# Where a graph kernel's first count matrix is built, and how its rows' beginnings are found

## The chip, the cores and the metric

The kernel runs on one core of one Trainium2 chip. Its metric is the device time of one execution in microseconds; of several runs the median is given. A profile shows one further execution, with each engine's instructions: PE (TensorE matmul; PEld is its weight load), DVE (VectorE), ACT (ScalarE), POOL (GpSimd) and SP (SyncE, which here only issues transfers).

## The reference, cut to what matters

A four-layer graph network on 6250 nodes and 100000 edges sorted by destination. Destinations are drawn as 6250 u^2, so the low nodes have by far the most edges.

```python
h = relu(layernorm(x))                                       # 6250 x 256
deg = segment_sum(ones, dst)
h1 = h @ W1_self + (segment_sum(h[src], dst) / max(deg, 1)) @ W1_neigh + b1     # 256 -> 512
hp = relu(h1 @ W2_pool + b2_pool)
h2 = h1 @ W2_self + segment_max(hp[src], dst) @ W2_neigh + b2
h3 = ((segment_sum(h2[src], dst) + h2) / (deg + 1)) @ W3_neigh + b3
h4 = h3 @ W4_self + (segment_sum(h3[src], dst) / max(deg, 1)) @ W4_neigh + b4
out = x + h4 @ W_fc + b_fc                                   # 6250 x 256
```

## The kernel before

Nodes are cut into 49 tiles of 128, edges into 782 columns of 128. Sums over edges are made in two ways. For the first eight tiles of destinations (H1 = 8, the hub) a **count matrix** A is built: how many edges go from each source to each destination; the sum is then a dense product of A with all 49 tiles of h, which lie in SBUF as Z1 (three bf16 parts of each number). For the other tiles (d = 8 to 48) each edge column is **gathered**: `sums` issues on POOL one indirect transfer per column (L386) from the table tab_h in DRAM into a ring of 14 buffers, PE multiplies it by a one-hot matrix in three matmuls (L404) into pg, and DVE adds pg, masked by M, to acc (L421, L423), of which there are three. When a tile's sum is whole, `done1` finishes it: deg and the mean (L818 to L822, the mean m1 on ACT), transposes, the product with Wa and Wb (L838, L841), and stores of tab_t and tab_p. Layer 2 begins with gathers from tab_p (L1144), and needs all of it.

`build` (L297 to L331) makes A for one tile. The tile's 128 destinations are 16 **windows** of 8. A window's edges lie one after the other in the sorted list and fill up to k_of[w] rows of 128 edges: 31 for the first window, 14 for the next, then 11, 9, 8, 8; 139 rows for tile 0, 67, 52, 48, 48, 43, 32, 32 for tiles 1 to 7. One row is one **run**: ACT makes a one-hot matrix of the source's place in its tile, by Abs and Relu (L309, L311), DVE a mask of source tile and destination (hm, L313), and PE multiplies them (L319). At the end of a window DVE takes the maximum (L323) and ACT copies the counts into A (L324).

A `Hub` is a list of such work: `advance(to)` emits items up to number `to`, and the one-hot matrices four runs (LOOK) ahead.

**The beginning of the program, the prologue** (L533 to L802), has to find where each window's rows begin. The row number of window beginnings is found by a two-step search: how many of 128 equal pieces of the edge list end before the window (cF), then a gather of that piece of dst (drow, L621) and a count of what lies under the window's first node (L625). The 384 beginnings (three columns of SN) are turned into a row by PE (L631, starts), spread on POOL over at_row with a span for each k (33 spans; L653, L655), and turned back by PE into columns of row beginnings (L659, pa, atF, atI): 7 columns of 128 rows, of which the first 4 (RB1 = 512 rows) belong to the hub's eight tiles. Then `window_rows(b)` gathers 128 rows of dst and of src (L676), converts and transposes them, and `window_keys` makes of them the keys: sk (minus the source's place in its tile) and mk (what the mask is compared with). The first 512 go to sk1 and mk1; layer 2 reads the others from stash_k.

Beside this the prologue normalises x in seven groups of seven tiles (`layer_norm`, L568 to L594): statistics on DVE (L574, L575), Sqrt and Relu on ACT (L578, L584), the three bf16 parts by ACT (L587), DVE (L588), POOL (L589) and DVE (L590), and a store into tab_h. x is loaded into three buffers (xt). `turn` and `tail_keys` prepare the sources and keys of the gathered edges, `products1` multiplies weights.

**Layer 1** then emits, in this order: all of build 0; and, in `sums`, 474 gathers, behind each of which the hub advances in proportion. The hub's list is dense product 0 merged with build 1, dense 1 with build 2, and so on to dense 7. It ends with the last gather.

The order in the program is not the order in an engine's queue: the framework plans each engine's queue ahead, from estimated durations, by when an instruction's inputs should be there and, among those ready, by its place in the program. On the chip each queue then runs in that fixed order.

The kernel finds out at run time whether the input has the assumed shape (`bad`); a general path is taken otherwise, which does not run here.

Of the kernel before, what the change touches and what calls it, by code (L numbers as in the profile page):

```python
# [9 lines left out]
F32 = mybir.dt.float32  # L10
BF16 = mybir.dt.bfloat16
F16 = mybir.dt.float16
F8 = mybir.dt.float8e4
I32 = mybir.dt.int32
AF = mybir.ActivationFunctionType
ALU = mybir.AluOpType
AX = mybir.AxisListType
PSUM = bass.MemoryType.PSUM
DRAM = bass.MemoryType.DRAM

P = 128
# [4 lines left out]
G = 4  # L26
BLOCKS = (52, 100, 220, 180, 130, 100)
MERGED = 3
Z_SIGMA = 5.0
WIN = 8  # L30
# [48 lines left out]
def fast_path(  # L79
# [15 lines left out]
    nc = tc.nc  # L95
    N, FI = x.shape
    E = src.shape[0]
    FH = W1_self.shape[1]
    FO = W_fc.shape[1]
    NT = (N + P - 1) // P  # L100
# [234 lines left out]
    class Hub:  # L335
# [9 lines left out]
        def add(self, work):  # L345
            for w in work:
                if isinstance(w, tuple):
                    self.hot_at.append(len(self.work))
                else:
                    w = (None, w)  # L350
                self.work.append(w)

        def left(self):
            return len(self.work) - self.done

        def advance(self, to):
# [9 lines left out]

    def sums(pool, psg, table, F, srcT, keyT, jb, h, done, deep, hub, wait=0, counts=0, todo=()):

# [24 lines left out]
        for g in range(g_of[h][0], NG):  # L393
            pg = bank(psg, "pg", "pg", (F + counts,))
            n = min(G, T - g * G)
            for k in range(n):
                j = g * G + k
                X = ring[:, j % deep, :]
                gather(j)
                if j + ahead < T:  # L400
                    one_hot(j + ahead)
                for part in (2, 0, 1):
                    c = counts if part == 2 else 0
                    nc.tensor.matmul(  # L404
                        pg[:, : F + c], hot[j], X[:, part * F : (part + 1) * F + c],
                        start=(k == 0 and part == 2), stop=(k == n - 1 and part == 1),
                    )
                del hot[j]
                at = j - j0 + 1
                if at > wait:  # L410
                    hub.advance(math.ceil(len(hub.work) * (at - wait) / (T - j0 - wait)))
                if todo and next(todo[0], None) is None:
                    todo.pop(0)
# [102 lines left out]
    nc.gpsimd.memset(Z1[:, :, 3 * FI :], 1.0)  # L516
    for d in range(H1, NT):
        last = d == NT - 1
        ends = (g_of[d][0] * G * P, EX if last else (g_of[d][1] + 1) * G * P,
                offs[b_of[d][0]], EX if last else offs[b_of[d][1] + 1])  # L520
        for k in range(4):
            nc.gpsimd.memset(lim[:, k, d : d + 1], float(ends[k]))
    w1pool = layer1.enter_context(tc.tile_pool(name="w1", bufs=1))
# [6 lines left out]
    sk1 = w1pool.tile([P, RB1], F32, name="sk1")  # L530
    mk1 = w1pool.tile([P, RB1], F32, name="mk1")

    with ExitStack() as pro:  # L533
# [18 lines left out]
        def load_x(g):  # L552
            xt = lp.tile([P, LG, FI], F32, name="xt", bufs=3)
            i0 = g * LG
# [9 lines left out]

        for g in range(3):
            load_x(g)
# [28 lines left out]


        ones_b = ep.tile([P, 1], BF16, name="ones_b")
        nc.vector.memset(ones_b, 1.0)
        iota_n = ep.tile([P, 3 * P], F32, name="iota_n")
        nc.gpsimd.iota(iota_n, pattern=[[WIN, 3 * P]], base=0, channel_multiplier=0,  # L600
# [16 lines left out]
        within = ep.tile([P, 3], F32, name="within")  # L617
        drows = dflat[0:EP].rearrange("(p t) -> p t", t=T)
        for c in range(3):
            row = ep.tile([P, T], I32, name="drow", bufs=1)  # L620
            nc.gpsimd.indirect_dma_start(  # L621
                out=row, out_offset=None, in_=drows,
                in_offset=bass.IndirectOffsetOnAxis(ap=cI[:, c : c + 1], axis=0),
            )
            nc.vector.tensor_scalar(row, row, SN[:, c, 1:2], 0.0, op0=ALU.is_lt, op1=ALU.add,  # L625
                                    accum_out=within[:, c : c + 1])
        nc.vector.scalar_tensor_tensor(SN[:, :, 0], cF, float(T), within,
                                       op0=ALU.mult, op1=ALU.add)
        pr_ = bank(psm, "pm", "pr_s", (3 * P,))
        for c in range(3):  # L630
            nc.tensor.matmul(pr_[:2, c * P : (c + 1) * P], SN[:, c, :], ident,  # L631
                             start=True, stop=True)
        starts = ep.tile([2, 3 * P], F32, name="starts")
        nc.vector.tensor_copy(starts, pr_[:2, :])


        room = ep.tile([1, NW], F32, name="room")
        i = 0
        while i < NW:
            n = sum(1 for w in range(i, NW) if k_of[w] == k_of[i])  # L640
            nc.gpsimd.memset(room[:, i : i + n], float(k_of[i] * P))
            i += n
        has = ep.tile([1, NW], F32, name="hasw")
        nc.vector.tensor_sub(has, starts[:1, 1 : NW + 1], starts[:1, :NW])
        nc.vector.tensor_tensor(has, has, room, op=ALU.is_gt)
        nc.vector.tensor_reduce(bad[:1, 1:2], has, AX.X, ALU.max)


        at_row = ep.tile([2, RB * P], F32, name="at_row")
        nc.gpsimd.memset(at_row, 0.0)  # L650
        nc.gpsimd.memset(at_row[:1, :], float(E))
        for r, w0, n, k in spans:
            nc.gpsimd.tensor_copy(at_row[:, r : r + n], starts[:, w0 : w0 + n])  # L653
            if k:
                nc.gpsimd.tensor_scalar(at_row[:1, r : r + n], at_row[:1, r : r + n],  # L655
                                        float(k * P), None, op0=ALU.add)
        pa = bank(psm, "pm", "pa", (RB, 2))
        for b in range(RB):
            nc.tensor.matmul(pa[:, b, :], at_row[:, b * P : (b + 1) * P], ident[:2, :2],  # L659
                             start=True, stop=True)  # L660
        atF = ep.tile([P, RB, 2], F32, name="atF")
        nc.vector.tensor_copy(atF, pa)
        atI = ep.tile([P, RB], I32, name="atI")
        nc.vector.tensor_copy(atI, atF[:, :, 0])


        sk = ep.tile([P, RB * P], F32, name="skf")
        mk = ep.tile([P, RB * P], F32, name="mkf")
        skI = ep.tile([P, RB * P], I32, name="skI")
        dw = ep.tile([P, RB * P], F32, name="dwf")  # L670

        def window_rows(b):
            got = []
            for flat in (dflat, sflat):
# [10 lines left out]
            for i in range(2):  # L685
                nc.tensor.transpose(pt[:, i, :], f[:, i, :], ident)
            c = slice(b * P, (b + 1) * P)
            nc.vector.tensor_copy(dw[:, c], pt[:, 0, :])
            nc.vector.tensor_copy(mk[:, c], pt[:, 1, :])

        def window_keys(c0, c1):
            c = slice(c0, c1)
            nc.vector.tensor_copy(skI[:, c], mk[:, c])
# [89 lines left out]
        steps = products1()  # L783
        turn()
        for b in range(RB1 // P):
            window_rows(b)
        window_keys(0, RB1)
        nc.vector.tensor_copy(sk1, sk[:, :RB1])
        nc.vector.tensor_copy(mk1, mk[:, :RB1])
        for g in range(NT // LG):  # L790
            layer_norm(g)
            if g + 3 < NT // LG:
                load_x(g + 3)
            next(steps, None)
            if RB1 // P + g < RB:
                window_rows(RB1 // P + g)
        for _ in steps:
            pass
        tail_keys()
        window_keys(RB1, RB * P)  # L800
        nc.sync.dma_start(stash_k[:, 0, :], sk)
        nc.sync.dma_start(stash_k[:, 1, :], mk)  # L802


    with ExitStack() as on:
        pst = on.enter_context(tc.tile_pool(name="pst1", bufs=1, space=PSUM))
        psm = on.enter_context(tc.tile_pool(name="psm1", bufs=1, space=PSUM))
        psg = on.enter_context(tc.tile_pool(name="psg1", bufs=2, space=PSUM))
        psb = on.enter_context(tc.tile_pool(name="psb1", bufs=2, space=PSUM))
        psd = on.enter_context(tc.tile_pool(name="psd1", bufs=2, space=PSUM))  # L810
# [5 lines left out]
        def done1(d, acc):  # L816
# [23 lines left out]
            for k in range(KI):  # L840
# [6 lines left out]

        As = [wk.tile([P, NT, P], F8, name=f"A{i}", bufs=1) for i in range(2)]
        keys = (sk1, mk1, 0)
        todo = []  # L850
        builds = [build(d, As[d % 2], keys, wk, psb) for d in range(H1)]
        denses = [dense(range(NT), lambda s, A=As[d % 2]: A[:, s, :], h0_row, FI, psd,
                        lambda acc, d=d: todo.append(done1(d, acc)), extra=1)
                  for d in range(H1)]
        work = list(builds[0])
        first = len(work)
        for d in range(H1):
            work += merged(denses[d], builds[d + 1]) if d + 1 < H1 else denses[d]
        hub = Hub(work)
        hub.advance(first)  # L860
        todo.append(segments())
        sums(wk, psg, tab_h, FI, srcT, keyT, JC * P, H1, done1, 14, hub, counts=1, todo=todo)
    layer1.close()

# [1102 lines left out]
```

## Time and profile before

| | |
|---|---|
| median of 3 runs | 3042.52 us (3040.0 to 3048.64) |
| profiled execution | 3044.61 us, span 3042.8 us |
| busy share of the span | PE 81%, PEld 46%, DVE 67%, ACT 30%, POOL 67% |
| POOL's gathers of layer 1 (L386 from tab_h) | 474, 0.95 us each, from 148.9 to 785.9 us |
| first gather of layer 2 (L1144) | 824.5 us |
| first dense matmul (L442) | 267.0 us |

A line of a timeline gives the start, the duration, engine, source line, operation, output and inputs with shape, and in brackets how long the engine stood idle just before and what ended that. A line of windows gives, for a stretch, its length and, for each engine, the busy time and the number of instructions; PEclk is the granted clock of TensorE as a share of full speed. Matmuls overlap, so their durations add up to more than their distances.

### The profile page before, as it was taken

The page shows a single profiled execution, that of the slowest core. Times are in us where ns is not written, and L with a number is a line of the kernel's source. Part 1 is how long each engine was busy: PE and PEld are TensorE (multiplying, and loading weights), DVE is VectorE, ACT ScalarE, POOL GpSimd, SP SyncE. Part 2 cuts the span into 40 slices and gives each one's busy share as a digit, 9 for nine tenths or more (in the row PEclk, how much of TensorE's full clock was granted, in tenths as well). Part 3 has the DMA queues.
Part 4 walks back from the last instruction along what each step waited for, and adds up shares of the span by engine and source line. Part 5 has one row for each costly group of instructions (what it writes and reads, how often), then busy time and mean ns, then how long its engine had stood idle before and what let it go on. Part 6 is the DMA issues. An engine that isn't in the chain of part 4 may idle for free. (4 is left out here: it accounts for less than half of the span.)

```text
span 3042.8 us, 41553 instructions
## 1 busy us (share of the span) xinstructions
PE 2459.1 (81%) x12699; PEld 1402.3 (46%) x12699; DVE 2039.5 (67%) x5161; ACT 905.7 (30%) x2383; POOL 2051.3 (67%) x2260
## 2 busy tenths in 40 slices
PE   1468999999778664767789994983699999799999
PEld 0234666666543321323334442431234444488888
DVE  4956767766378788666779997987266676444433
ACT  2557766765255666421111110100000001000000
POOL 5274777776366676777767777765477777677775
PEclk9787999999999776788899997996799999899999
DMA  6454667776599999999989998987799999878886
GB/s 191 148 158 134 202 206 213 213 214 206 165 387 354 334 390 376 363 387 387 371 275 318 323 315 280 310 287 223 291 368 385 383 381 375 310 234 239 247 239 193
DMA packets 380021, 865.41 MB, mean 284 GB/s; under 512 B 58078, under 2 KB 151238, under 8 KB 379756
## 3 DMA queue, kind: packets, MB, share of 16 engines
q0 software_dynamic: 146560, 514.74, 51.8%
q1 hardware_dynamic: 175144, 292.49, 25.9%
q10 hardware_dynamic: 58084, 55.44, 5.8%
q8 instruction: 103, 1.69, 0.2%
q14 instruction: 130, 1.06, 0.1%
HBM read 610.65 MB, written 252.60 MB: 284 GB/s over the span
## 5 line engine op out<-in xcount | busy, mean ns | idle before, releaser
L1144 POOL DMA_INDIRECT X<-tab_p,srcIf x782 | 839.8, 1074 | 384.5 <-issue 161.5
L404 PE MATMUL pg<-ring,hot 128*128 128x256 bf16 (+2 forms) x3390 | 682.6, 310 | 78.3 <-DMA ring<-tab_h,srcT 34.8
L442 PE MATMUL pd<-zt,ac 128*128 128x256 bf16 (+1 forms) x3462 | 566.8, 299 | 21.6 <-DMA ac<-tab_a 12.2
L386 POOL DMA_INDIRECT ring<-tab_h,srcT x474 | 451.5, 952 | 195.8 <-PE pg L404 76.9
L404 PEld LDWEIGHTS <-hot 128*128 128x128 bf16 x3390 | 332.7, 99 | 303.1 <-issue 134.9
L442 PE MATMUL pd<-r,ae 128*128 128x512 bf16 x1536 | 378.5, 396 | 96.5 <-DVE acc L941 45.2
L386 POOL DMA_INDIRECT ring<-tab_r,srcE x342 | 330.6, 967 | 146.5 <-PE pg L404 63.6
L442 PEld LDWEIGHTS <-ac 128*128 128x128 fp8e4 x3462 | 339.4, 98 | 151.7 <-issue 21.0
L311 ACT ACTIVATE hs<-ht,onef 128x128 bf16<-128x128 bf16 x781 | 292.3, 395 | 305.3 <-PE pb L319 303.6
L319 PE MATMUL pb<-hm,hs 128*128 128x392 bf16 x781 | 257.4, 380 | 152.4 <-ACT A L324 109.4
L386 POOL DMA_INDIRECT ring<-tab_s,srcE x314 | 298.7, 951 | 112.8 <-issue 60.5
L423 DVE SCALAR_TENSOR_TENSOR acc<-pg,M,acc 128x257 f32<-128x257 f32 (+2 forms) x518 | 273.0, 561 | 151.4 <-PE pg L404 150.6
L1149 DVE SCALAR_TENSOR_TENSOR X<-X,samef 128x512 f32<-128x512 f32 x391 | 292.0, 748 | 97.6 <-DMA X<-tab_p,srcIf 84.0
L1149 DVE SCALAR_TENSOR_TENSOR X<-X,samef,X 128x512 f32<-128x512 f32 x385 | 287.2, 747 | 92.9 <-DMA X<-tab_p,srcIf 46.1
L442 PEld LDWEIGHTS <-ae 128*128 128x128 fp8e4 x1536 | 155.1, 101 | 330.4 <-issue 153.2
L382 DVE TENSOR_SCALAR hot<-iota_bf,keyE 128x128 bf16<-128x128 bf16 x656 | 153.5, 268 | 132.2 <-PE pg L404 126.0
L1083 PE MATMUL pm_prf<-unf,hTf 128*128 128x512 f32 x392 | 199.6, 637 | 2.8 <-ACT hTf L1074 2.8
L319 PEld LDWEIGHTS <-hs 128*128 128x128 bf16 x781 | 81.9, 105 | 249.5 <-issue 165.3
L442 PE MATMUL pd<-Z,A 128*128 128x256 bf16 (+1 forms) x1176 | 189.1, 274 | 0.3 <-ACT A L324 0.2
L313 DVE TENSOR_SCALAR hm<-iota_w,mk 128x392 bf16<-128x392 f16 x461 | 154.5, 344 | 46.0 <-PE pb L319 44.8
L324 ACT ACTIVATE A<-pb 128x392 fp8e4<-128x392 f32 x288 | 139.3, 486 | 147.7 <-DVE most L323 113.8
L323 DVE TENSOR_REDUCE most<-pb 128x1 f32<-128x392 f32 x288 | 160.8, 559 | 32.6 <-PE pb L319 31.9
(288 smaller groups left out, 2881.9 us busy)
## 6 DMA issues: line engine op xcount, KB each, us to landing
runb<-X SPq DMA_DIRECT2D x208, 512.0 KB
runb<-X SPq DMA_DIRECT2D x183, 256.0 KB
tab_r<-r SPq DMA_DIRECT2D x49, 384.0 KB
tab_a<-A SPq DMA_DIRECT2D x18, 784.0 KB
tab_t<-th SPq DMA_DIRECT2D x49, 256.0 KB
tab_p<-hpf SPq DMA_DIRECT2D x49, 256.0 KB
th<-tab_t ACTq DMA_DIRECT2D x49, 256.0 KB
X<-tab_p,srcIf POOLq DMA_INDIRECT x782
```

The source lines that it names most:

```text
L311: nc.scalar.activation(hots[0], t, AF.Relu, bias=one, scale=-1.0)
L313: nc.vector.tensor_scalar(hots[1], iota_w, mk[:, r : r + 1], None, op0=ALU.is_equal)
L319: nc.tensor.matmul(hold[0], hots[0], hots[1], start=(k == 0), stop=(k == k_of[w] - 1))
L323: nc.vector.tensor_reduce(most[:, w : w + 1], hold[0], AX.X, ALU.max)
L382: nc.vector.tensor_scalar(hot[j], iota_b, keyT[:, j - jb : j - jb + 1], None, op0=ALU.is_equal)
L386: nc.gpsimd.indirect_dma_start(out=ring[:, j % deep, : 3 * F], out_offset=None, in_=table, in_offset=bass.IndirectOffsetOnAxis(ap=srcT[:, ...
L404: nc.tensor.matmul(pg[:, : F + c], hot[j], X[:, part * F : (part + 1) * F + c], start=(k == 0 and part == 2), stop=(k == n - 1 and part == 1),
L423: nc.vector.scalar_tensor_tensor(acc[d], pg, m, acc[d], op0=ALU.mult, op1=ALU.add)
L442: nc.tensor.matmul(hold[0][:, : F + c], a, z[:, part * F : (part + 1) * F + c], start=(s == ss[0] and part == 2), stop=(s == ss[-1] and pa ...
L1083: nc.tensor.matmul(pm, hT[:, c, :], un[:, c, :], start=False, stop=(c == KH - 1))
L1144: nc.gpsimd.indirect_dma_start(out=X[:, k, :], out_offset=None, in_=tab_p, in_offset=bass.IndirectOffsetOnAxis(ap=srcI[:, t : t + 1], axis=0),
L1149: nc.vector.scalar_tensor_tensor(X[:, k, :], prev, same[:, t : t + 1], X[:, k, :], op0=ALU.mult, op1=ALU.max,)
```

## The change

Four things are different.

1. The search gathers the first of the three columns and counts it; the row beginnings of the first four columns are made from it alone. Row beginnings no longer pass through a row on one partition. A matrix win_of says for each row which window it belongs to; from it DVE makes for each column c of SN a selection matrix (1 where the row's window is that column's entry), and PE multiplies it with SN; a further matmul adds k times 128 for rows behind the first of a window, or the list's end for rows of no window. The second and third columns, and the last three columns of rows, follow after the first keys. The check that each window has room comes behind the second normalisation. The memsets of lim come behind `turn`, which itself comes later.
2. The keys sk1 and mk1 are made in place; stash_k gets only the others.
3. build 0 becomes a Hub `made` before the prologue. Behind each of the seven normalisations it advances by a seventh of its first 45 per cent (62 of 139 runs). Its matrix, one-hot buffers and PSUM banks are therefore there in the prologue, and x has two buffers in place of three.
4. In layer 1 the rest of build 0 heads the hub's list in `sums`, in place of standing ahead of the gathers, and the hub's pace is set so that it ends 24 gathers before the last.

```diff
+PART0 = 45
...
+        def rest(self):
+            at = set(self.hot_at[: self.hot])
+            return [(None if i in at else w[0], w[1])
+                    for i, w in enumerate(self.work) if i >= self.done]
...
-                    hub.advance(math.ceil(len(hub.work) * (at - wait) / (T - j0 - wait)))
+                    hub.advance(math.ceil(len(hub.work) * (at - wait) / (T - j0 - wait - rest)))
...
+    bpool = layer1.enter_context(tc.tile_pool(name="build1", bufs=1))
+    psb1 = layer1.enter_context(tc.tile_pool(name="psb1", bufs=2, space=PSUM))
+    As = [bpool.tile([P, NT, P], F8, name="A0", bufs=1)]
+    made = Hub(build(0, As[0], (sk1, mk1, 0), bpool, psb1))
+    part0 = len(made.work) * PART0 // 100
...
-            xt = lp.tile([P, LG, FI], F32, name="xt", bufs=3)
+            xt = lp.tile([P, LG, FI], F32, name="xt", bufs=2)
...
+        for r, w0, n, k in spans:
+            nc.gpsimd.iota(win_of[:, r : r + n], pattern=[[1, n]], base=w0,
+                           channel_multiplier=0, allow_small_or_imprecise_dtypes=True)
+            nc.gpsimd.memset(later[:, r : r + n], float(k * P))
...
+        def select(c):
+            nc.vector.tensor_scalar(sel[c], win_of[:, sel_at[c] : sel_at[c] + sel[c].shape[1]],
+                                    float(-c * P), pidx, op0=ALU.add, op1=ALU.is_equal)
+        select(0)
...
+        def row_begins(b0, b1, cs):
+            pa = bank(psm, "pm", "pa", (RB, 2))
+            for b in range(b0, b1):
+                for c in cs:
+                    nc.tensor.matmul(pa[:, b, :], sel[c][:, b * P - sel_at[c] : (b + 1) * P - sel_at[c]],
+                                     SN[:, c, :], start=(c == cs[0]), stop=False)
+                nc.tensor.matmul(pa[:, b, :], later[:, b * P : (b + 1) * P], unit,
+                                 start=False, stop=True)
+            nc.vector.tensor_copy(atF[:, b0:b1, :], pa[:, b0:b1, :])
+            nc.vector.tensor_copy(atI[:, b0:b1], atF[:, b0:b1, 0])
...
-        turn()
+        begins(0, 1)
+        row_begins(0, RB1 // P, (0,))
         for b in range(RB1 // P):
             window_rows(b)
-        window_keys(0, RB1)
-        nc.vector.tensor_copy(sk1, sk[:, :RB1])
-        nc.vector.tensor_copy(mk1, mk[:, :RB1])
+        window_keys(sk1, mk1)
+        select(1)
+        select(2)
+        begins(1, 3)
+        row_begins(RB1 // P, RB, (1, 2))
+        turn()
...
         for g in range(NT // LG):
             layer_norm(g)
-            if g + 3 < NT // LG:
-                load_x(g + 3)
+            if g + 2 < NT // LG:
+                load_x(g + 2)
             next(steps, None)
             if RB1 // P + g < RB:
                 window_rows(RB1 // P + g)
+            made.advance(part0 * (g + 1) // (NT // LG))
+            if g == 1:
+                check_room()
...
-        work = list(builds[0])
-        first = len(work)
+        work = []
         for d in range(H1):
             work += merged(denses[d], builds[d + 1]) if d + 1 < H1 else denses[d]
-        hub = Hub(work)
-        hub.advance(first)
+        hub = Hub(made.rest() + work)
         todo.append(segments())
-        sums(wk, psg, tab_h, FI, srcT, keyT, JC * P, H1, done1, 14, hub, counts=1, todo=todo)
+        sums(wk, psg, tab_h, FI, srcT, keyT, JC * P, H1, done1, 14, hub, counts=1, todo=todo, rest=24)
```

## The prediction

> **What bounds the kernel now.** I read the page first. Its chain of waits goes back only to 2121 us, so it says nothing about the beginning, where this change sits; that part has to be read from windows and from the queues' timelines. The windows in 25 us steps (columns: length, then busy time and count of PE, PEld, DVE, ACT, POOL, then the granted TensorE clock, DMA share, GB/s) show four regimes:
>
> ```profile
> 50.00:75.00 25.00, 3.63 (x12) 2.57 (x12) 8.56 (x18) 5.23 (x8) 17.18 (x32) 1.00 0.34 107
> 125.00:150.00 25.00, 7.63 (x22) 2.76 (x22) 25.00 (x116) 19.39 (x57) 3.79 (x4) 0.55 0.41 151
> 175.00:200.00 25.00, 15.46 (x78) 8.41 (x78) 14.07 (x48) 12.77 (x41) 19.02 (x20) 0.84 0.56 155
> 250.00:275.00 25.00, 19.07 (x65) 7.59 (x63) 13.10 (x38) 23.64 (x78) 0.97 (x2) 0.59 0.14 51
> 475.00:500.00 25.00, 24.73 (x180) 17.77 (x178) 19.79 (x72) 19.45 (x53) 18.91 (x21) 1.00 0.67 192
> ```
>
> At 50 to 75 us nobody works: DVE waits. From 100 us to the end of the prologue DVE is full. At 175 us layer 1's gathers run at POOL's rate (20 in 25 us, 1.25 us each) and PE has room. At 250 us the gathers have stopped and ACT is full. From 275 us on PE and POOL are both at their limit. The timelines of POOL, DVE and ACT name the turning points:
>
> ```profile
> 58.22 0.17 DVE L662 COPY atF<-pa 128x14 f32<-128x14 f32 x1 [14.82 <-PE pa L659]
> 59.42 3.82 POOL L676 DMA_INDIRECT wrow<-dflat,atI  x1 [0.67 <-DVE nb L582]
> 92.42 0.42 DVE L789 COPY mk<-mkf 128x512 f32<-128x512 f32 x1
> 140.83 2.02 DVE L590 TENSOR_TENSOR Z<-xt,Z 128x1792 bf16<-128x1792 f32 x1
> 148.88 0.97 POOL L386 DMA_INDIRECT ring<-tab_h,srcT  x1 [9.24 <-DMA tab_h<-Z]
> 267.08 0.93 ACT L822 ACTIVATE m<-acc,rmeanf 128x256 f32<-128x256 f32 x2
> 270.54 0.95 POOL L386 DMA_INDIRECT ring<-tab_h,srcT  x1 [23.99 <-PE pg L404]
> 824.51 0.97 POOL L1144 DMA_INDIRECT X<-tab_p,srcIf  x1 [37.63 <-DMA tab_p<-hpf]
> ```
>
> DVE stands 14.8 us at L662 for the row beginnings. The keys of the first 512 rows (sk1, mk1) are there at 92.8 us. The first gather waits for the last store of tab_h, behind the last L590. Build 0 then keeps ACT until 267 us; the copies m1 of finished sums stand behind it, with them the three acc buffers, the ring, and the gathers (24 us at 270.5). The last gather issues at 785.9 us, 37.6 us before layer 2's first. Layer 1's stage is thus 824.5 - 148.9 = 675.6 us; all behind it waits for tab_p and should move with it.
>
> **Part 1, the row beginnings.** Removed: three gathers of drow through one buffer (first issued 12.8 us, SN ready 36.3), and on POOL 33 copies and 31 additions into at_row, from 41.17 to 57.12 us. In their place one gather decides: it lands at 20.2, its count L625 takes 1.03, then eight small f32 matmuls (the L659 row: eight in 2.09 us) and two copies of 0.2: about 24.5 us instead of 59.1 for the first window gather. From it to mk1 took 92.8 - 59.4 = 33.4 us; the same again gives 58 us. Added: three selections, 512, 384 and 384 wide; the trace has no f16 to f32 form, but L699, two operations over 512 f32, takes 0.42 and over 384 0.35: 1.1 us of DVE; twice that if the form is slow. On POOL 33 iotas and 33 one-row memsets: L208's iota is 0.13, L205's 128x392 0.45, the lim memsets are 164 in 5.46, so about 27 x 0.13 + 6 x 0.24 + 33 x 0.04 = 6.3 us (up to 10, if each costs the 0.27 of a small addition on L655). They stand ahead of iota_n where the 5.46 us of lim stood, and iota_n (7.45) is not needed before dlast at 10.88: nothing to 1 us. The lim memsets go behind the window gathers, where POOL has slack (9.9 of 25 us busy at 75); without it, they delay one middle copy L589 by up to 5.5 us.
>
> **Part 2, the first 62 runs of build 0 in the prologue** (45% of 139, some nine behind each layer normalisation). A run costs ACT two activations at one per 0.29 us in a row (L309, L311 at 136 to 155 us): 0.585 us, 36 us in all. From 58 to 138 us ACT is busy some 34 of 80 now (5.2, 4.7, 16.0 and 8 in the windows), so it fits. DVE: 62 x 0.24 (L313, fifteen in 3.55) = 14.9, three reductions L323 of 0.56: 1.7, selections 1.1, less the copies L788 and L789 of 0.84: **+16.9 us**. DVE has 91.4 busy in the first 138 us, so 46.6 idle, of which 14.8 is the L662 wait that falls away and 7.5 (69.8 us) and 5.1 (89.0) are waits for window rows that now come while normalisations can fill them. If only the first is gained, the prologue grows by 2 us; if all are, it shrinks by 10. Should none be, it is 17.
>
> Against it stand two x buffers where there were three. The last group: statistics from 124.0, last L590 done at 142.8, 18.8 us; its load, 7 us for the first group (2.3 to 9.4), 11 for the last; and a chunk's 5.3 us of ACT and 2.2 of DVE may fall into the chain. A buffer is then held 33 to 37 us, with two of them a group each 17 to 18 us. Before, the L590s went from 38.6 to 140.8, 17.0 each. So the buffers allow what was there, hardly better: first store at 40, plus 6 x 17, plus the 6.1 us from last L590 to first gather, 148. Between 138 and 151 I take **147** for the first gather, 2 us earlier.
>
> Two rules of the Trainium skill speak against the move. The GPSIMD Engine Reference (8. Key points) says that GpSimd shares its SBUF interface with VectorE and suffers when the latter works in a two-port mode or with two SBUF inputs; L313, 16-bit with one source, may be of the first kind. The seven L589 took 1.67 to 2.08 us here; at the worst each for 0.4 more, 3 us, by the row nothing. I take nothing. TensorE: Matmul & The Clock Gate (Part 1: The HAM clock gate) says that the array runs at half rate, 1.2 GHz, without some 3.4 us of sustained work. Where it counts is the beginning of layer 1, below.
>
> **Part 3, layer 1.** 77 runs are left, followed by 392 dense and 322 other runs: 791 items over 474 - 24 = 450 gathers, 1.76 each. Build 0 is over at gather 44, so after 44 x 1.25 = 55 us, where it now takes until 267 us, 118 us after the first gather. ACT then needs 1.76 x 0.585 = 1.03 of each 1.25 us, and finished sums come from gather 36 on: the 24 us stall goes. PE needs, by the distance between starts in its timeline at 800 to 807 us, at full clock: 0.33 for a gather's three matmuls, 0.33 for a dense item, 0.163 for a run (392 columns in proportion to 0.33 for 3 x 257), 4.0 for the tile's end (0.33 + 0.23 + 1.72 + 1.72). In the first 44 gathers it has 0.33 + 1.76 x 0.163 = 0.62 each. By the row, the clock was 0.77 to 0.84 in this regime: 0.8 us, hidden. By the page's half rate (2.4 GHz halved, so 771 columns in 0.64 and 1.76 x 392 in 0.57) 1.22 of 1.25: just hidden. The sum is the same, with no margin by the page.
>
> Middle, 406 gathers: 0.33 + 392/406 x 0.33 + 322/406 x 0.163 + 45/406 x 4.0 = 1.22 us. The same prices give 500 us for what PE did between 275 and 808, where it took 533 (20 of it idle), so 1.25 to 1.30. POOL's floor is 1.25. Between them I take **1.29**, near the 1.30 that the gathers kept from 270 to 786: 524 us. Last 24: only sums and their ends, 24 x 1.25 = 30. After the last issue no dense backlog is left (22 us of it before, last L404 at 807.7): landing 3, one tile end of 10 instead of two in 16.7: 13. Sum 55 + 524 + 30 + 13 = 622, against 675.6.
>
> **The sum.** 147 + 622 = 769 for layer 2's first gather, 55.5 us earlier. The profiled execution had 3044.6 us, span 3042.8: it becomes 2989. It lay 2 us above the median of the runs, hence **2987**. The stores into stash_k that lose 512 of 896 columns, and the check of room, which now comes behind group 1, I cost at nothing: SP has slack at 109 us, and the verdict is read only ahead of the last layer; uncovered, its four DVE operations are 2.3 us.
>
> **The rivals.** *The prologue grows* (0.22). For: DVE is full from 100 us, and each queue's order is planned ahead, so a window row that lands late still stops everything. Against: the longest wait is gone. At 21 us per group: 40 + 126 + 6 = 172, plus 622, 794: 3012.
>
> *Both floors are reached* (0.12): first gather at 138, pitch 1.25 throughout, 605 us: 743, 81 us earlier, 2961. For: gathers kept exactly 20 per 25 us from 300 to 700. Against: PE was 99% busy there.
>
> *Slower* (0.10): two x buffers with no overlap. A load can't start until the last subtraction of the group two before, and that stands behind masks of build 0 which wait for PE and ACT. At 29 us per group 40 + 174 + 6 + 622 = 842, 17.5 later: 3060. It decides from (824.5 - 622 - 46)/6 = 26 us per group. Against: the last three L590s come 6 to 15 us after the one before.
>
> *It doesn't do what it says* (0.06): the order in which PE takes dense and sums leaves the backlog as it was and the pitch rises to 1.38, so the stage ends where it did: 3040.
>
> **How the numbers follow.** The forecast has 0.50, and 2970 to 3005 by its own bounds (first gather 138 to 155, pitch 1.25 to 1.31). The range takes in the grown prologue and the floors, 2958 to 3040, and leaves out the slower case and the far end of the faster. A change of 0.3%, 9 us, is about what a measurement of this kernel can tell from none. Faster beyond it are the forecast, the grown prologue and the floors, 0.84 less the part of the second that eats its gain: 0.82; within it 0.07; slower 0.11.
>
> **What would show it.** Right: the first window gather near 25 us; no long DVE wait for the row beginnings; first ring gather at 138 to 155; no gap of gathers; the first dense matmul some 55 us behind the first gather (267 us before); the last tile's end within 15 us of the last gather; layer 2 at about 769. Wrong: stores of tab_h on average more than 20 us apart, DVE or ACT waiting in the prologue for window rows or masks; gathers over 1.35 us apart in the middle; or a later stage that gives the gain back.

## The result, and the profile after

The changed kernel takes **3006.64 us** (median of four runs, 3002.8 to 3009.09) where the kernel before takes 3043.07 beside it: a ratio of **0.9885 [0.9867, 0.9902]**, 36 us less. The forecast was 2987, with 2958 to 3040 around it; the sign was right, and about two thirds of the forecast gain came. The profiled execution had 3004.22 us with a span of 3002.3, 40.5 us below the span before, and layer 2's first gather stands 39.7 us earlier: what lies behind layer 1 moved as one piece.

The windows of the changed kernel, in the columns used before (length, busy time and count of PE, PEld, DVE, ACT, POOL, then clock, DMA share, GB/s):

```profile
50.00:75.00 25.00, 22.72 (x72) 10.07 (x72) 22.00 (x69) 21.12 (x67) 3.69 (x3) 1.00 0.66 210
125.00:150.00 25.00, 10.73 (x25) 2.80 (x26) 25.00 (x100) 21.92 (x66) 1.83 (x2) 0.50 0.33 121
175.00:200.00 25.00, 17.49 (x78) 8.92 (x78) 13.46 (x46) 13.51 (x44) 18.91 (x21) 0.71 0.56 158
250.00:275.00 25.00, 22.89 (x149) 15.32 (x148) 16.01 (x56) 16.40 (x47) 18.90 (x21) 0.99 0.64 189
```

The hole at 50 to 75 us is filled: DVE is busy 22.0 of 25 us there, against 8.6. The hole of POOL at 250 to 275 is gone too: 21 gathers in place of two (0.97 us of POOL). In between nothing was won: from 100 to 150 us DVE is as full as before.

The turning points, from the timelines of POOL and DVE of the changed kernel:

```profile
10.32 5.68 POOL L833 MEMSET lim<- 1x1 f32 x164
16.52 1.10 POOL L651 DMA_INDIRECT drow<-dflat,cI  x1 [0.52 <-DVE wrongf L758]
28.67 0.17 DVE L675 COPY atF<-pa 128x8 f32<-128x8 f32 x1 [3.69 <-PE pa L673]
30.14 0.95 POOL L709 DMA_INDIRECT wrow<-dflat,atI  x1 [2.16 <-DVE mv L582]
50.71 0.68 DVE L735 TENSOR_TENSOR mk<-mk,dwf 128x512 f32<-128x512 f32 x1
143.48 2.01 DVE L597 TENSOR_TENSOR Z<-xt,Z 128x1792 bf16<-128x1792 f32 x1
151.79 0.98 POOL L393 DMA_INDIRECT ring<-tab_h,srcT  x1 [9.85 <-issue]
784.81 0.97 POOL L1187 DMA_INDIRECT X<-tab_p,srcIf  x1 [26.48 <-DMA tab_p<-hpf]
```

The window gathers start at 30.1 us (59.4 before), DVE's wait for the row beginnings is 3.69 us (14.82), and the keys mk1 are there at 51.4 (92.8). So the row beginnings come 29 us earlier and the keys 41 us earlier, and yet the first ring gather is 2.9 us *later*: 151.8 against 148.9. The whole gain lies behind it. Its 474 gathers run from 151.8 to 757.4 us without a stall (the longest wait is 2.3 us), 1.28 us apart (148.9 to 785.9 before, 1.35 on average with the stall), and from the last of them to layer 2's first it takes 27.4 us, where it took 38.6. Of the 39.7 us, 2.9 were lost in the prologue, 31.4 were won over the gathers and 11.2 behind the last one.

What DVE does in the prologue is seen in its groups between 50 and 143 us (busy time, then mean ns of one):

```profile
L314 DVE TENSOR_SCALAR hm<-iota_w,mk 128x392 bf16<-128x392 f16 x84 | 25.2, 351 | 0.0
L581 DVE BATCH_NORM_STATS2 st<-xt 128x6 f32<-128x256 f32 x35 | 13.3, 397 | 0.3 <-DMA xt<-in_x 0.3
```

These are 84 masks, not 62: the planner drew more than 20 runs of the part that is written behind the gathers forward into this stretch. And DVE waits only 0.3 us for x. It looks as if DVE were the bound of this prologue and its masks the reason. That was my first theory of the miss, and it fell.

### The profile page after: what moved, and what is told of

It reads as the page before. It is cut to its first block, busy times and chain, and to the rows that moved or that the text cites. A ratio compares the mean times of both kernels' runs of the same rounds, so it can differ in the third digit from the quotient of the medians.

```text
span 3002.3 us, 41497 instructions
## 1 busy us (share of the span) xinstructions
PE 2449.3 (82%) x12637; PEld 1403.4 (47%) x12719; DVE 2039.3 (68%) x5169; ACT 904.1 (30%) x2383; POOL 2035.2 (68%) x2260
## 5 line engine op out<-in xcount | busy, mean ns | idle before, releaser
L411 PE MATMUL pg<-ring,hot 128*128 128x256 bf16 (+2 forms) x3375 | 675.3, 309 | 79.2 <-DMA ring<-tab_h,srcT 36.2
L320 PE MATMUL pb<-hm,hs 128*128 128x392 bf16 x781 | 254.7, 375 | 150.3 <-ACT A L325 111.5
L310 ACT ACTIVATE ht<-iota_bf,sk 128x128 bf16<-128x128 bf16 x461 | 172.2, 395 | 6.5
```

What stands on the lines that cost most here:

```text
L310: nc.scalar.activation(t, iota_b, AF.Abs, bias=sk[:, r : r + 1])
L320: nc.tensor.matmul(hold[0], hots[0], hots[1], start=(k == 0), stop=(k == k_of[w] - 1))
L411: nc.tensor.matmul(pg[:, : F + c], hot[j], X[:, part * F : (part + 1) * F + c], start=(k == 0 and part == 2), stop=(k == n - 1 and part == 1),
```

## The experiments

Theory A: the first gather is late because DVE carries some 85 masks, 0.30 us each, ahead of the last store of tab_h. Theory B: it is late because two x buffers set the pace of the layer normalisations, and the masks lie in time that DVE has anyway. The experiments ran together on another chip, on which the kernel before takes 3453.88 us (3419.73 to 3475.4, 29 runs) and the gathers of layer 1 stand 1.75 to 1.84 us apart, so of their times only the ratios count, and lengths of layer 1 are compared among them alone. In the prologue the chips agree well enough for comparison (first window gather at 30.4 to 30.7 us with the new row beginnings, 30.1 above). The last of the four kernels below has the whole prologue of the change: its first gather is at 151.0 us, so on this chip that is the number to compare with. Neither the kernel before nor the changed kernel has a trace from this chip.

**The row beginnings alone.** Build 0 stays whole and ahead of the gathers, with three x buffers and the old pace:

```diff
-    As = [bpool.tile([P, NT, P], F8, name="A0", bufs=1)]
-    made = Hub(build(0, As[0], (sk1, mk1, 0), bpool, psb1))
...
-            xt = lp.tile([P, LG, FI], F32, name="xt", bufs=2)
+            xt = lp.tile([P, LG, FI], F32, name="xt", bufs=3)
...
-            made.advance(part0 * (g + 1) // (NT // LG))
...
-        hub = Hub(made.rest() + work)
+        hub = Hub(builds[0] + work)
+        hub.advance(len(builds[0]))
...
-        sums(wk, psg, tab_h, FI, srcT, keyT, JC * P, H1, done1, 14, hub, counts=1, todo=todo, rest=24)
+        sums(wk, psg, tab_h, FI, srcT, keyT, JC * P, H1, done1, 14, hub, counts=1, todo=todo, rest=0)
```

> The new row beginnings alone: build 0 stands whole ahead of the gathers as before the change, x has its three buffers, the hub's pace is the old one. Twelve masks stand ahead of the last store of tab_h in DVE's queue (six before the change, 85 with all of it). Theory A, the prologue is DVE's: with the 14.8 us wait gone and no masks added the first gather comes at 128 to 136 us, layer 1 then takes its old 676 us, and the whole 3022 to 3032 us. Rival B, the chain through the x buffers sets the first gather and the wait only hid in it: first gather at 146 to 150, the whole at 3040 to 3044.

Measured: ratio 0.9933 [0.9906, 0.996]. The timeline of POOL and the window behind it:

```profile
131.32 0.97 POOL L393 DMA_INDIRECT ring<-tab_h,srcT  x1 [9.47 <-DMA tab_h<-Z]
278.42 0.94 POOL L393 DMA_INDIRECT ring<-tab_h,srcT  x1 [36.50 <-PE pg L411]
...
250.00:275.00 25.00, 16.33 (x40) 4.01 (x40) 15.43 (x46) 25.00 (x85) 0.00 (x0) 0.50 0.00 1
```

The first gather is at 131.3 us, 17.6 ahead of the kernel before (whose trace is from the first chip). That is what the new row beginnings, with the keys made in place, are worth if nothing else is touched; the stores of tab_h then follow each other at 11.5 us on average. Build 0 still stops the gathers, for 36.5 us here, with ACT full and POOL empty. The prologue is as theory A has it, and B as it was put for this run (the x buffers set the first gather even when there are three) is out. That two buffers set it is still open, as there are three here.

**All but the row beginnings.** The old search through at_row, with the share in the prologue, two buffers and the new pace:

```diff
-        begins(0, 1)
-        row_begins(0, RB1 // P, (0,))
...
-        select(1)
-        select(2)
-        begins(1, 3)
-        row_begins(RB1 // P, RB, (1, 2))
...
+        for c in range(3):
+            row = ep.tile([P, T], I32, name="drow", bufs=1)
...
-            if g == 1:
-                check_room()
```

> All of the change but the new row beginnings: these are made on POOL as before, one drow buffer, starts, at_row. Theory A: DVE gets its 15 us wait back and the keys come some 35 us later, while 86 masks still stand ahead of the last store: first gather at 162 to 175, the whole at 3016 to 3030. Rival B (DVE is full from 76 us on anyway and would only be full later): first gather within 4 us of 152, the whole at 3004 to 3010.

Measured: ratio 0.9935 [0.9906, 0.9963], and

```profile
56.66 0.17 DVE L669 COPY atF<-pa 128x14 f32<-128x14 f32 x1 [14.82 <-PE pa L666]
179.37 0.98 POOL L393 DMA_INDIRECT ring<-tab_h,srcT  x1 [9.29 <-DMA tab_h<-Z]
...
1032.95 0.97 POOL L1155 DMA_INDIRECT X<-tab_p,srcIf  x1 [24.86 <-DMA tab_p<-hpf]
```

The first gather is 4 us beyond A's bracket, 23 us beyond the latest that B allowed, and 28 us behind that of the kernel with the whole prologue, so the early keys are needed: masks of build 0 start only at 82.8 us, and DVE is busy just 7.1 of the 25 us from 50 to 75. The third group's x was asked for at 39.5 us, but its statistics stand in DVE's queue among the window rows and masks, from 71.9 to 91.7 us, and its store comes 51.8 us behind the second's. From there on the stores follow at 15.4 us each (111.80 to 173.40), the pace of the changed kernel. Beside its late prologue, this kernel has the shorter layer 1: 853.6 us from its first gather to layer 2's, against 910.8 with the row beginnings alone. Each part by itself is worth 0.7%, one ahead of the first gather, the other behind it. Together they gave 1.1% on the first chip.

**No mask ahead of the last store.** PART0 is 0, and the masks of the remaining runs compare with a copy of mk1 that needs the last group of Z1, so that they can't be drawn forward:

```diff
-PART0 = 45
+PART0 = 0
...
+        mk1b = wk.tile([P, RB1], F32, name="mk1b", bufs=1)
+        nc.vector.scalar_tensor_tensor(mk1b, Z1[:, NT - 1, FI : 3 * FI], 0.0, mk1,
+                                       op0=ALU.mult, op1=ALU.add)
+        mk1s.append(mk1b)
```

> After the change, with no run of build 0 ahead of the last store of tab_h: the share is 0 and the masks compare with a copy of mk1 that waits for that store's data, so that the planned order can't draw them forward. 0 masks in place of 85, two x buffers. Theory A: 85 masks and five reductions, 28 us of DVE, are gone, first gather at 122 to 132; layer 1 has 92 runs more to do and its first dense matmul comes 90 us behind the first gather in place of 62; the stage takes 648 to 662 in place of 633, the whole 2994 to 3012. Rival B, two x buffers bind: first gather at 145 to 152, the whole at 3016 to 3032.

Measured: ratio 0.9911 [0.9879, 0.9943]. Its windows, and the rows of two groups' way through the buffers from the queues of SP, DVE, ACT and POOL:

```profile
75.00:100.00 25.00, 7.06 (x23) 3.35 (x22) 23.09 (x92) 11.28 (x19) 3.85 (x2) 0.68 0.32 108
100.00:125.00 25.00, 0.00 (x0) 0.00 (x0) 23.65 (x113) 10.89 (x18) 2.70 (x3) 0.50 0.55 177
125.00:142.30 17.30, 0.00 (x0) 0.00 (x0) 7.53 (x20) 5.44 (x9) 2.48 (x2) 0.50 0.31 107
```

```profile
100.33 0.36 SPq L601 DMA_DIRECT2D tab_h<-Z  x1
100.74 0.56 SPq L569 DMA_DIRECT2D xt<-in_x  x1
...
109.19 0.43 DVE L584 BATCH_NORM_STATS2 st<-xt 128x6 f32<-128x256 f32 x1
...
116.45 3.55 ACT L594 ACTIVATE xt<-xt,nb,rs 128x256 f32<-128x256 f32 x7 [0.53 <-DVE fhalf L478]
120.03 1.69 ACT L597 CAST Z<-xt 128x1792 bf16<-128x1792 f32 x1
122.03 2.02 DVE L598 TENSOR_TENSOR xt<-xt,Z 128x1792 f32<-128x1792 f32 x1
124.11 1.68 POOL L599 CAST Z<-xt 128x1792 bf16<-128x1792 f32 x1 [8.94 <-DVE fixIf L511]
125.83 2.02 DVE L600 TENSOR_TENSOR Z<-xt,Z 128x1792 bf16<-128x1792 f32 x1 [1.71 <-POOL Z L599]
...
142.29 2.03 DVE L600 TENSOR_TENSOR Z<-xt,Z 128x1792 bf16<-128x1792 f32 x1 [1.78 <-POOL Z L599]
150.25 0.97 POOL L395 DMA_INDIRECT ring<-tab_h,srcT  x1 [8.00 <-DMA tab_h<-Z]
```

Here theory A falls. All masks are gone from the stretch (the first one is at 145.1 us), and the first gather is at 150.3, not at 122 to 132: 0.8 us ahead of the kernel of this chip that has the masks (151.0). The second fence shows what sets the pace: the load of a group goes out when the last subtraction of the group two before has ended, 0.4 us behind that group's store in the same queue; its first statistics come 8.5 us later; then statistics, Relu, the three parts one after the other on ACT, DVE, POOL, DVE. From load to last part: 100.7 to 127.9, 27.1 us. Over all five groups that are loaded so, a buffer is held for 35.6, 33.0, 28.2, 27.1 and 25.0 us, 29.8 on average; two buffers share it, which is 14.9 us per group, where 15.1 was measured. The last parts stand at 87.70, 98.25, 116.34, 125.83 and 142.29, two groups in 26 to 29 us. DVE's full row did not show a bound: with the masks gone, the planner put small operations of a later stage (L476 to L518, lists of rows to mend) in their place, and from 100 to 125 us DVE was still busy 23.7 of 25 us, while PE had nothing at all to do. When these ran out, from 125 us to the start of the last part, it was busy 7.5 of 17.3 us, and the last group still came 16.5 us behind the one before. The first two holds are longer by more than load and stages: in the first the statistics begin only 15.4 us behind the load, and in the second it takes 24.2 us from them to the end of the last part, where the last group takes 15.0. So the masks are excluded as the cause; that DVE's other work took part in the pace up to 125 us is not.

In layer 1 this kernel pays for it: its first dense product comes 171.7 us behind the first gather, not 90, and there is again a stall, of 24.3 us, that ends at 338.6 us, with ACT busy 22.4 of the 26.6 us before. On that chip's slower gathers, its layer 1 is nevertheless within 4 us of the next kernel's (870.7 and 873.9).

What isn't tried: the direct test of theory B, three buffers against two with all else equal, for instance two buffers in the kernel with the row beginnings alone. That kernel has the same layer normalisations, three buffers, the new row beginnings and stores 11.5 us apart (the last four parts begin at 91.41, 101.14, 110.05 and 123.28); it differs from this one in the buffers and in build 0, which has no mask ahead of the last store here and some a few us ahead of it there. B is thus supported by these two runs and by the 15.4 us of the one before, but not shown by itself; A is excluded by one.

**The old pace of the hub.** The items are spread over all 474 gathers, the last 24 included:

```diff
-        sums(wk, psg, tab_h, FI, srcT, keyT, JC * P, H1, done1, 14, hub, counts=1, todo=todo, rest=24)
+        sums(wk, psg, tab_h, FI, srcT, keyT, JC * P, H1, done1, 14, hub, counts=1, todo=todo, rest=0)
```

> After the change with the hub's old pace: it ends with the last gather and not 24 ahead of it. If the pace shortens the stage's end: from the last gather to layer 2's first 34 to 40 us in place of 27, the last gather some 3 us earlier, the whole 3010 to 3016. Rival: PE has the same work in all and no idle time, so that the order at the end is worth nothing: within 3 us of the change, 3004 to 3010.

Measured: ratio 0.9922 [0.9892, 0.9953]. POOL's rows, and the end of PE's timeline:

```profile
151.02 0.97 POOL L393 DMA_INDIRECT ring<-tab_h,srcT  x1 [9.68 <-issue]
1024.95 0.97 POOL L1187 DMA_INDIRECT X<-tab_p,srcIf  x1 [37.62 <-DMA tab_p<-hpf]
```

```profile
1008.52 0.49 PE L449 MATMUL pd<-Z,A 128*128 128x257 bf16 x3
...
1017.00 1.98 PE L884 MATMUL pm_hp<-Wa,th 128*128 128x512 f32 x4 [1.46 <-ACT th L879]
1018.82 1.88 PE L887 MATMUL pm_hp<-Wb,th 128*128 128x512 f32 x4
```

POOL's wait is 37.62 us, as in the kernel before (37.63), where the kernels with the new pace had 24.8 to 26.5: dense products run until 1008.5, 22 us behind the last gather, and two tile ends follow them. So the pace alone is worth 11 to 13 us behind the last gather. The rival has it that this is paid for ahead of it, by a later last gather with the new pace. The kernel with the old row beginnings lets one see that: it has the new pace, about as many runs done before its first gather (92 against 90), and its first dense product as far behind it (84.8 and 84.9 us). Its gathers stand 1.750 us apart, against 1.766 with the old pace, so nothing was paid, and its layer 1 is 20.3 us shorter (853.6 against 873.9). By these two traces the rival falls on this chip, where PE has more room (busy 18.3 of 25 us at 475 to 500, against 24.7 in the kernel before on the first). That the last gather would come 3 us earlier with the old pace did not happen. In the time of the whole the step can't be told, since the intervals of all four kernels overlap.

## Why the prediction was right, and where it was off

**Row beginnings, 24.5 us: 30.1.** The work was priced well: the 33 iotas and 33 memsets took 3.42 to 9.60 us on POOL, 6.2 us with the waits in it (6.3 predicted), and from the first window gather to mk1 it took 21 us, less than the 33 of before. What failed first is "the lim memsets go behind the window gathers". Written behind, they were planned ahead: having no inputs, they were ready, so 5.7 us of them run from 10.3 us, and the gather of drow stands behind them at 16.5 (12.8 before). Not all of the 3.7 us are theirs: its row number cI was ready at 13.7 us rather than 12.5, as all three selections, two of them also written behind, ran 1.98 us on DVE from 8.84, ahead of the first statistics. The count of drow began at 23.1 us, where 20.2 was forecast: 2.9 of the missing 5.6 us. The second slip is in the matmuls. The "eight in 2.09 us" of L659 were four matmuls, since each of these f32 matmuls has two records; the new scheme has eight, and its 16 records took 4.2 us (24.46 to 28.63). On top of it DVE counted the second column (1.02 us) between the two copies.

**First gather, 147: 151.8.** It was right to a few us by luck: two errors cancel. The step said first store at 40, six groups of 17, and 6.1 behind. It came to 53.4 (the keys now stand on DVE ahead of the first group's parts, with the last mk row at 50.7), six groups of 15.4, and 6.3 behind the end of the last part. The pace was put down to DVE and buffers together; without a mask it is 15.1. The buffers are held 27 to 33 us (33.2, 29.3, 26.9, 31.1 and 30.2, 30.1 on average), not 33 to 37, and half of that is the pace. The +16.9 us of DVE were 62 masks; 84 ran. The kernel without them has its first gather 0.8 us earlier than the one with them on the same chip, so they cost hardly more than that (other work took part of their place). The slower rival, two x buffers without overlap at 29 us per group, and the grown prologue at 21, were both far from it; yet the slower rival's suspect, the buffers, fits the runs best: the kernel with three has its first gather at 131 us.

**First dense product 55 us behind the first gather: 62.** By the first gather 91 of 139 runs had been done rather than 62, so the smaller rest should have ended sooner. The term that failed is 1.76 items per gather: the 48 runs left went over 49 gathers, about one each, and in PE's timeline from 195 to 207 us most of them stand singly between the matmuls of two gathers, where PE waits 0.2 to 1.1 us at a time for the ring. Why they were queued so and not closer these runs don't show. No gather waited for it.

**The middle, 1.29 us a gather: 1.28.** 151.8 to 757.4 is 605.6 us, where 55 + 524 + 30 = 609 were predicted. The stall of 24 us is gone for the reason given: finished sums found ACT free (13.5 of 25 us busy from 175 to 200); both kernels that keep most of build 0 for after the prologue stall again, for 36.5 and 24.3 us. The clock weighed in this part was granted at 0.71 from 175 to 200 us, PE was busy 17.5 of 25 us, and POOL kept its 1.25: between the price by the row and that by the half rate of the Trainium skill (TensorE: Matmul & The Clock Gate, Part 1), both of which hid it. The other rule of the skill, on SBUF shared by GpSimd and VectorE (GPSIMD Engine Reference, 8. Key points), was looked for on the wrong engine. POOL's copies took no longer with ten times as many masks beside them: L596 1.68 to 1.95 us, those of before 1.67 to 2.08. But DVE's instructions did:

```profile
42.54 1.69 POOL L596 CAST Z<-xt 128x1792 bf16<-128x1792 f32 x1
42.23 2.09 DVE L716 CAST wrowf<-wrow 128x128 f32<-128x128 int32 x1 [0.18 <-DMA wrow<-sflat,atI]
82.04 1.65 DVE L589 SCALAR_TENSOR_TENSOR nb<-mv,rs 128x7 f32<-128x7 f32 x1
110.52 1.07 DVE L314 TENSOR_SCALAR hm<-iota_w,mk 128x392 bf16<-128x392 f16 x1
```

The same three forms take 0.18 to 0.23, 0.15 to 0.17 and some 0.3 us elsewhere in this prologue, and each of these three ends within 0.2 us of the end of a copy (44.23, 83.68 and 111.47 us). By that, DVE's full row holds waits of this kind too. What they cost in the end was not tested; the prediction looked for a loss at the copies alone and took nothing.

**Behind the last gather, 13 us: 27.4.** This is the term that cost most, 14.4 of the 15.8 us by which layer 2's first gather missed 769; 4.8 came from the first gather, and the middle gave 3.4 back. The step was "landing 3, one tile end of 10". The trace has three. PE's timeline of the changed kernel behind the last gather at 757.4:

```profile
758.66 2.03 PE L411 MATMUL pg<-ring,hot 128*128 128x256 bf16 x17
...
763.05 1.98 PE L884 MATMUL pm_hp<-Wa,th 128*128 128x512 f32 x4
764.87 1.88 PE L887 MATMUL pm_hp<-Wb,th 128*128 128x512 f32 x4
...
768.03 1.98 PE L884 MATMUL pm_hp<-Wa,th 128*128 128x512 f32 x4
769.85 1.88 PE L887 MATMUL pm_hp<-Wb,th 128*128 128x512 f32 x4
...
774.01 0.44 PE L877 MATMUL pt_m<-identf,m 128*128 128x128 f32 x2 [1.50 <-ACT m L868]
775.16 2.94 PE L884 MATMUL pm_hp<-Wa,th 128*128 128x512 f32 x4 [0.72 <-ACT th L879]
777.90 2.66 PE L887 MATMUL pm_hp<-Wb,th 128*128 128x512 f32 x4
```

The ring holds 14 gathers, and when the last is issued PE still has nearly all of them before it: 41 matmuls, three per gather. Spread over these are the last tiles' ends, whose products take 3.9, 3.9 and 5.6 us (the last at a lower clock; see the last section). I had removed the 22 us of dense backlog and had not asked how many gathers, and ends of tiles, a full ring leaves behind its last issue. That these ends follow each other on PE is read from the trace; a kernel without two of them was not run, so how much each is worth is open. The four experiments fit it: with the new pace the stretch is 25.7 and 25.8 us, with dense products up to the end 38.6 both times.

**The sum.** 2989 was predicted for the profiled execution, 3004.2 came, and the 15 us are the 15.8 of layer 2's first gather: behind it the change moved everything as expected.

## What to carry to other kernels

A queue that is full in the profile isn't always the bound: where a planner fills waits with whatever is ready, take the suspected work away and see whether the end moves. Count the buffers' round trip (load, all stages, release) and divide it by their number before giving one of them away: here the kernel with the third buffer had its first gather 19 us ahead of the one with two and no mask, about as much as the faster search won (17.6), though the buffer alone was not tested. And work that has no inputs, or whose inputs are ready, does not stay where it is written; what must not run early needs an input that comes late.

## What I had not expected of the hardware

The last tile's products took 2.94 and 2.66 us, those of the two tiles ahead of it 1.98 and 1.88, in the same form, after PE had stood 1.5 and 0.7 us for ACT. In the kernel without masks ahead of the store the last tile's waits were nearly the same (1.51 and 0.72 us), and its products took 1.98 and 1.88. The granted clock goes with it: 0.72 over these products (774.5 to 780.6 us) in the first, 1.00 (1012.5 to 1017) in the second, and 3.86 us divided by 0.72 is 5.4. Why the clock fell after the same waits in one and not in the other isn't shown. On the second chip, the same gathers stood 1.75 to 1.84 us apart (the 1.84 with the stall of 36.5 us in it) rather than 1.28, with a DMA share of 0.48 at 475 to 500 us against 0.67; the profile gives no single cause, and I leave it open.
